# First sequence's gates and gate-weight sums placed inside the last FP4 down products, and its gate matrix by seven products

## The chip, the cores and the metric

The kernel runs as one launch on one core of a Trainium2 chip. The metric is the time of that launch on the device, in microseconds (us); the number given for a kernel is the median of several runs. For the kernel before that is 986.02 us, from three runs between 985.76 and 986.28 us.

## The reference, cut to what matters

Two layers follow each other on 2048 rows (two sequences of 1024 tokens) of 512 features. The first is linear attention and an FFN whose weights are packed FP4. The second is gated linear attention and an FFN that only the better half of the tokens passes. Each of the four steps ends in `x = layernorm(x + step(x))`. The change is at the seam between the FP4 FFN and the gated attention:

```python
# FP4 FFN (down part):      y = (silu(gate) * up) @ w_down.T ; y / rms(y)
# gated attention, per sequence:
q = softmax(x @ Wq.T); k = sigmoid(x @ Wk.T); v = x        # 32 features each
gf = log_sigmoid(-k)                                       # decay gates
o = gla_chunk(q, k, v, gf)                                 # chunked scan with state S
go = o @ Wog.T + x @ Wig.T                                 # the gate matrix, 512 x 1024
on = o * rsqrt(mean(o * o) + 1e-5) * g_norm_w
out = (on * silu(go)) @ Wo.T
```

`go` is one product of the 1024-wide pair (x, o) with the pair (Wig, Wog).

## The kernel before, in words

Rows are worked in four blocks of 512 tokens (blocks 0 and 1 are the first sequence, 2 and 3 the second). Weights and activations are fp32, and all products run on TensorE; a product of two 2 x 2 block matrices is done with seven block products instead of eight wherever the sums that this needs can be made beforehand by VectorE or GpSimd (Strassen's way, in Winograd's form). One fp32 matmul of the program shows as two MATMUL records in the trace.

**The FP4 stage (L688 to L944).** For each block `scaled_sums` (L690) makes gate and up from the unpacked weights `wgu` (45 KB in each partition), and `down` (L734) multiplies the result with `wdn` in products P1, P2, P5, P4, P6, P7, P3 and a rest P8, each ended by VectorE adds into `y`. The down products of a block lie inside the gate and up products of the next one; those of block 3 have nothing to lie in and stand alone, from about 509 to 552 us. The loop after `Wog` is loaded hands them out in seven portions, and between the portions it puts the transposes of block 1 (`turn`) and the 64 small matmuls `logits(0)` (L661), whose bank `lp` holds q and k of the first sequence before their nonlinearities. `Wig` and `Wog` are loaded at 494.6 and 509.3 us into rooms of their own. `old.rest()` and `now.rest()` (L855 on) are the row normalisations of blocks 2 and 3.

**The gated attention (from L945).** Here `fp4` is closed and its memory goes to new pools: `w34` (with `w1` and four rooms B0 to B3), `jk`, and `wk` (stage 3). `Gates` (L984) turns `lp` into q, k, the log decay `l` and its suffix sums `e`: activations Exp, Exp, Exp, Ln, Exp on ScalarE, seven VectorE operations between them, one matmul `ep` (L1008) and the product `kd` (L1011). It uses tiles of `wk`, so that it can't begin before the FP4 stage is over. `scores` (L1015) makes for one block the decays `ex` from a matmul `cp`, transposes q and k (`tp`), builds the masked score matrix A through `sc` and `sk`, a per-block decay through the small matmul `dp` (L1055), and the states S through four `up` matmuls. `attend` (L1083) makes o^T in 28 or 32 pairs of small matmuls (`op`), which ScalarE copies out and squares. `rms` (L1106) gives the row factors.

**The gate matrix.** Block 0 takes `plain_gate` (L1127): eight matmuls of 512 columns for each of four row groups, four with `Wig` (spread as fillers in `scores(0)`, which calls them by `beside`) and four with `Wog` after `attend`. Each group ends in a Silu and one VectorE operation. Blocks 1 to 3 take `gate` (L1144), which does the same by seven products of eight 256-column matmuls, with sums of the weights (`sums_of_gate`, L973, four VectorE operations of 1024 elements), of x and o (`x_sum`, `o_sum`, `other_sums`). In the trace these weight sums lie between 583 and 593 us. `finish_by_seven` and `finish` multiply by `W1o` and add to x; `scored_rows` normalises and scores the rows, `route` ranks them.

**What sets the order.** The order in the program is not the order on the engines: a scheduler places every instruction by its own estimate of when its inputs are there, and `tc.issue_after(ins)` holds a group back behind an instruction. Each engine then works its list strictly in order. PSUM banks are handed out in rings (`mm` and `acc`, four banks each here), so a matmul can also wait for the reader of the bank's last tile.

Of the kernel before, what the change touches and what calls it, by code (L numbers as in the profile page):

```python
# [10 lines left out]
F32 = mybir.dt.float32  # L11
# [62 lines left out]
def body(ctx: ExitStack, tc: tile.TileContext, a: dict, out: bass.AP):  # L74
# [147 lines left out]
    wgu = wfp4.tile([P, KC, 2 * I_FF], F32R, name="wgu")  # L222
# [446 lines left out]

    with tc.tile_pool(name="s2", bufs=1) as wk2:  # L670
# [137 lines left out]
        class Normed:  # L808
# [12 lines left out]
            def squares(self, part):  # L821
                for i in part:
                    nc.scalar.activation(junk, self.y[:, i], AF.Square, accum_out=self.ms[:, i : i + 1])

            def power(self):
                ms = self.ms
                nc.gpsimd.tensor_scalar(ms, ms, 1.0 / C, 1e-6, ALU.mult, ALU.add)
                nc.gpsimd.tensor_tensor(ms, ms, const("mhalf"), ALU.pow)
# [26 lines left out]
            def rest(self):  # L855

                for i in range(4):
                    x = x_t[self.blk][:, i]
                    nc.vector.scalar_tensor_tensor(x, self.y[:, i], self.ms[:, i : i + 1], x, ALU.mult, ALU.add)
                    row_stats(self.mv[:, i], x)  # L860
                    yield
                layernorm(x_t[self.blk], self.mv)
# [56 lines left out]
        load_w(Wog, "WogT")  # L919
        rings["mm"], rings["acc"] = range(4), range(4, 8)  # L920
# [3 lines left out]
        for n, steps in enumerate((11, 12, 10, 12, 10, 10, 14)):  # L924
# [4 lines left out]
            if n == 2:  # L929
                lp = logits(0)  # L930
        now.squares(range(4))
        now.power()
# [8 lines left out]
    w1 = w34.tile([P, KC, DFF], F32, name="w1")  # L941
    nc.sync.dma_start(out=w1, in_=a["w1"].rearrange("(k p) f -> p k f", p=P))
    load_w(W1o, "W1oT")
    nc.sync.dma_start(out=rw, in_=a["rw"].to_broadcast([P, C]))  # L944
    nc.sync.dma_start(out=b2, in_=a["b2"].to_broadcast([P, C]))  # L945
# [3 lines left out]

    def part(i, shape, name):  # L950

        return w34.tile([P, *shape], F32, tag=f"B{i}", name=name)
# [8 lines left out]


    gA11, gA12, gA21, gA22 = (
        w.rearrange("p k (m e c) -> p k m e c", e=2, c=P)[:, :, :, e] for e in range(2) for w in (Wig, Wog)
    )
    gsums = [part(i, [2, KC, 256], f"gsums{i}") for i in range(3)]
    gS1, gS2, gS4 = (
        gsums[i // 2][:, i % 2].rearrange("p k (m c) -> p k m c", c=P) for i in range(3)
    )
    T1, T2, T4 = gsums[1][:, 1], gsums[2][:, 0], gsums[2][:, 1]  # L970
    gS3 = gA21

    def sums_of_gate():  # L973
        nc.vector.tensor_add(gS1, gA21, gA22)
        nc.vector.tensor_sub(gS2, gS1, gA11)
        nc.vector.tensor_sub(gS3, gA11, gA21)
        nc.vector.tensor_sub(gS4, gA12, gS2)

# [5 lines left out]
    class Gates:  # L984


        def __init__(self, lp):
            lg = lp.rearrange("p (i d) -> p i d", d=64)
            q, k, l, e = (wk.tile([P, 8, 32], F32, tag=n, name=n) for n in ("q3", "k3", "l3", "e3"))
            kd = wk.tile([P, 8, 4, 32], F32, tag="kd", name="kd")  # L990
            self.q, self.k, self.l, self.kd = q, k, l, kd

            nc.scalar.activation(k, lg[:, :, 32:], AF.Exp, scale=-1.0)
            nc.vector.tensor_scalar_add(k, k, 1.0)
            nc.vector.reciprocal(k, k)
            nc.scalar.activation(l, k, AF.Exp)
            nc.scalar.activation(l, l, AF.Ln, bias=const("one"))
            red = sp.tile([P, 8], F32, tag="red", name="red")
            nc.vector.tensor_reduce(red, lg[:, :, :32], AX.X, ALU.max)
            nc.vector.tensor_sub(q, lg[:, :, :32], red.unsqueeze(2).to_broadcast([P, 8, 32]))  # L1000
            nc.scalar.activation(q, q, AF.Exp)
            den = sp.tile([P, 8], F32, tag="den", name="den")
            nc.vector.tensor_reduce(den, q, AX.X, ALU.add)
            nc.vector.reciprocal(den, den)
            nc.vector.tensor_mul(q, q, den.unsqueeze(2).to_broadcast([P, 8, 32]))

            ep = mm_bank("ep")
            nc.tensor.matmul(ep[:, :256], const("suf"), l.rearrange("p i d -> p (i d)"), start=True, stop=True)  # L1008
            nc.scalar.activation(e.rearrange("p i d -> p (i d)"), ep[:, :256], AF.Exp)

            nc.vector.tensor_mul(  # L1011
                kd, e.unsqueeze(2).to_broadcast([P, 8, 4, 32]), k.unsqueeze(2).to_broadcast([P, 8, 4, 32])
            )

    def scores(blk, gates, beside=None):  # L1015

        part = slice(4 * (blk % 2), 4 * (blk % 2) + 4)

        def flat(x):
            return x[:, part].rearrange("p i d -> p (i d)")  # L1020

        cp = mm_bank("cp")[:, : 3 * P]
        nc.tensor.matmul(cp, flat(gates.l), const("cm"), start=True, stop=True)
        ex = wk.tile([P, 4, P], F32, tag="ex", name="ex")
        nc.scalar.activation(ex[:, :3].rearrange("p e t -> p (e t)"), cp, AF.Exp)
        nc.scalar.activation(ex[:, 3], cp[:, :P], AF.Exp, scale=-1.0)
        tp = mm_bank("tp")
        nc.tensor.transpose(tp[:, :P], flat(gates.q), ident)  # L1030
        nc.tensor.transpose(tp[:, P : 2 * P], flat(gates.k), ident)
# [6 lines left out]

        last = sp.tile([P, 4], F32, tag="own", name="last")
        nc.vector.tensor_scalar_mul(last, own, ex[:, 2, P - 1 :])  # L1040
# [12 lines left out]
        dp = mm_bank("dp")  # L1053
        with tc.issue_after(beside(0)) if beside else contextlib.nullcontext():
            nc.tensor.matmul(dp[:, :4], const("quads"), last, start=True, stop=True)  # L1055
        decay = sp.tile([P, 4], F32, tag="decay", name="decay")
        nc.vector.tensor_copy(decay, dp[:, :4])
        sc = mm_bank("sc")
        with tc.issue_after(beside(1)) if beside else contextlib.nullcontext():
            nc.tensor.matmul(sc, km, qm.rearrange("p i t -> p (i t)"), start=True, stop=True)  # L1060
# [22 lines left out]
    def attend(blk):  # L1083

        A, qi = tri[blk]
        o = oT[blk] = wk.tile([P, KC, 512], F32, tag="oT", name="oT")
# [27 lines left out]
    def x_sum(blk):  # L1114
        nc.vector.tensor_sub(T1, xT[blk][:, :, 256:], xT[blk][:, :, :256])

    def o_sum(blk):
        nc.vector.tensor_sub(T2, oT[blk][:, :, 256:], T1)

    def other_sums(blk):  # L1120
        x, o = xT[blk], oT[blk]
        nc.vector.tensor_sub(x[:, :, 256:], o[:, :, 256:], x[:, :, 256:])
        nc.vector.tensor_sub(T4, o[:, :, :256], T2)

    banks, last_3 = [], [None]

    def plain_gate(m, first):  # L1127

        cut = slice(m * P, (m + 1) * P)
        if first:  # L1130
            banks.append(acc_bank("go"))
            for k in range(KC):
                ins = nc.tensor.matmul(banks[m], Wig[:, k, cut], xT[0][:, k], start=k == 0, stop=False).ins
            return ins
        else:
            for k in range(KC):
                nc.tensor.matmul(banks[m], Wog[:, k, cut], oT[0][:, k], start=False, stop=k == KC - 1)
            if m == 0:
                uT[0] = place_w(3, "uT")
            sil = wk.tile([P, 512], F32, tag="sil", name="sil", bufs=2)  # L1140
            nc.scalar.activation(sil, banks[m], AF.Silu)
            nc.vector.scalar_tensor_tensor(uT[0][:, m], oT[0][:, m], gw[:, m : m + 1], sil, ALU.mult, ALU.mult)

    def gate(blk):  # L1144


        u = uT[blk] = uT[0]
        c = u.rearrange("p (m e) (s t) -> p m e s t", e=2, s=2)
        c11, c12, c21, c22 = (c[:, :, e, s] for e in range(2) for s in range(2))
        x = xT[blk]  # L1150

        def product(ps, w, b, half, first):
            with tc.issue_after(last_3[0]):
# [25 lines left out]
        nc.scalar.copy(c11, product(one, gA11, x, 0, True))  # L1179
        yield  # L1180
        p5 = product(two, gS1, T1, 0, True)
        yield
        nc.scalar.copy(c22, p5)
        yield
        nc.scalar.copy(c12, product(one, gS2, T2, 0, False))
        p2 = product(acc_bank("go"), gA12, oT[blk], 0, True)
        yield nc.vector.tensor_add(c11, c11, p2).ins
        p7 = product(one, gS3, x, 1, False)
        yield nc.vector.tensor_add(c22, c22, p7).ins
        nc.vector.tensor_add(c12, c12, product(two, gS4, oT[blk], 1, False))  # L1190
        yield end(0)
        nc.scalar.activation(c21, product(one, gA22, T4, 0, False), AF.Silu)
# [3 lines left out]
    def sums_of_W1o():  # L1196
        W1oT = part(3, [4, 512], "W1oT")
# [217 lines left out]
    def finish_ffn(w2, h):  # L1415
# [59 lines left out]
        def steps(b):  # L1475
# [4 lines left out]
            c11 = wk.tile([P, 512], F32, tag="c11", name="c11")  # L1480
# [91 lines left out]
    gates = Gates(lp)  # L1572

    def fillers(h):

        turn(2, (2 * h, 2 * h + 1))
        plain_gate(2 * h, True)
        return plain_gate(2 * h + 1, True)

    scored = scores(0, gates, fillers)  # L1580
    with tc.issue_after(scored):
        for _ in ending:
            pass
        sums_of_gate()
        x_sum(1)
    for blk in range(NB):
# [146 lines left out]
```

## Time and profile before

| what | us |
|---|---|
| median of the runs shown | 986.02 |
| the profiled execution's own time | 985.74 |
| its span, first to last instruction | 983.8 |
| TensorE matmul busy | 967.1 (98%) |
| VectorE busy | 697.6 (71%) |
| ScalarE busy | 290.3 (30%) |
| GpSimd busy | 302.9 (31%) |
| block 3's last down product ends, the stage changes | 551.65 |
| the first product of `finish_by_seven` for block 0 begins | 611.07 |

The page of the profile gives busy time of each engine and the costliest groups. The waits view lists for each engine which line waited for which. The timeline gives, for a window, merged runs of one kind of instruction: its start, how long it ran, engine, line, operation, `out<-in` by tile names, shape, count, and in brackets the idle time before it and what ended that. PE is TensorE, DVE VectorE, ACT ScalarE, POOL GpSimd, SP the queue that starts DMAs.

### The profile page before, as it was taken

Reading aid. Unit: us, or ns where it says so; the run is one execution under the profiler, and the core shown is the slowest. Engines: PE = TensorE matmul, PEld = TensorE weight load, DVE = VectorE, ACT = ScalarE, POOL = GpSimd, SP = SyncE. Lnnn points to the kernel's source line nnn. Section 1 sums busy time; section 2 is a strip of 40 time slices with the busy share of each in tenths; the row PEclk is TensorE's granted clock in tenths of the full one; section 3 lists DMA queues with packets and bytes.
Section 4 is the critical chain, followed back from the end, with each engine's and each line's share of the span. In section 5 each row is a group of like instructions: output and inputs, shape, how many; then the busy total and the mean of one; then the engine's idle time right before and its main releaser. Section 6 shows DMA issues by size and latency. Waiting matters only on the chain. (4 is left out here: it accounts for less than half of the span.)

```text
span 983.8 us, 11753 instructions
## 1 busy us (share of the span) xinstructions
PE 967.1 (98%) x4373; PEld 768.5 (78%) x4373; DVE 697.6 (71%) x1340; ACT 290.3 (30%) x496; POOL 302.9 (31%) x276
## 2 busy tenths in 40 slices
PE   9999999999999999999999999999999999999996
PEld 6668876785888888888889656979768588888885
DVE  3569986987975686686672566565897795789644
ACT  2344323333542272263240442132221123220000
POOL 1110282005887265575565022001032011000022
PEclk9999999999999999999999999999999999999999
DMA  9632222100000000000020500000004302140011
GB/s 333 194 88 74 87 69 64 49 1 1 1 1 1 1 1 1 1 11 1 0 86 1 224 1 1 1 1 1 1 33 139 128 17 70 44 171 1 1 43 43
DMA packets 25979, 48.85 MB, mean 50 GB/s; under 512 B 4684, under 2 KB 6732, under 8 KB 25411
## 3 DMA queue, kind: packets, MB, share of 16 engines
q1 hardware_dynamic: 23283, 42.98, 13.2%
q0 software_dynamic: 1920, 4.22, 1.1%
q10 hardware_dynamic: 720, 0.92, 0.3%
q8 instruction: 34, 0.56, 0.2%
q14 instruction: 22, 0.18, 0.1%
HBM read 39.70 MB, written 10.52 MB: 51 GB/s over the span
## 5 line engine op out<-in xcount | busy, mean ns | idle before, releaser
L181 POOL TENSOR_TENSOR rs<-rs,table 128x4 f32<-128x4 f32 (+1 forms) x21 | 20.3, 967 | 301.3 <-DVE rs L180 301.0
L709 DVE SCALAR_TENSOR_TENSOR gate<-gatep,scale,gate 128x512 f32<-128x512 f32 x123 | 91.5, 744 | 7.4 <-PE gatep L698 6.9
L709 DVE SCALAR_TENSOR_TENSOR up<-upp,scale,up 128x512 f32<-128x512 f32 x112 | 83.2, 743 | 0.2
L698 PE MATMUL gatep<-x1Th,wgu 128*128 128x512 f32 x176 | 73.1, 415 | 0.6 <-DVE x1Tl L212 0.6
L698 PE MATMUL upp<-x1Th,wgu 128*128 128x512 f32 x176 | 70.4, 400 | 0.1
L698 PE MATMUL gatep<-x1Tl,wgu 128*128 128x512 f32 x176 | 69.6, 395 | 0.0
L698 PE MATMUL upp<-x1Tl,wgu 128*128 128x512 f32 x176 | 69.5, 395 | 0.0
L703 ACT ACTIVATE gate<-gatep,scale 128x512 f32<-128x512 f32 x41 | 28.3, 690 | 112.1 <-PE gatep L698 105.7
L745 PE MATMUL P<-wdn,h 128*128 128x256 f32 x256 | 60.5, 379 | 0.0
L898 POOL TENSOR_TENSOR h<-up,gate 128x512 f32<-128x512 f32 x30 | 38.6, 1286 | 69.6 <-ACT gate L897 64.5
L745 PEld LDWEIGHTS P<-wdn,h 128*128 128x128 f32 x256 | 48.5, 190 | 6.7
L1103 POOL TENSOR_TENSOR sum<-sum,sq 128x512 f32<-128x512 f32 x12 | 18.0, 1499 | 101.6 <-issue 77.1
L367 PE MATMUL xk<-pair,x 128*128 128x512 f32 x96 | 42.7, 592 | 0.0
L188 DVE BATCH_NORM_STATS2 st<-x 128x6 f32<-128x512 f32 x64 | 41.9, 677 | 0.4
L698 PEld LDWEIGHTS upp<-x1Th,wgu 128*128 128x128 f32 x176 | 33.0, 188 | 10.6 <-DVE up L709 2.4
L698 PEld LDWEIGHTS gatep<-x1Th,wgu 128*128 128x128 f32 x176 | 33.1, 188 | 8.8 <-DVE gate L709 1.1
L698 PEld LDWEIGHTS upp<-x1Tl,wgu 128*128 128x128 f32 x176 | 33.1, 188 | 7.6 <-issue 0.2
L698 PEld LDWEIGHTS gatep<-x1Tl,wgu 128*128 128x128 f32 x176 | 33.1, 188 | 6.9
L1463 PE MATMUL yp<-w,h 128*128 128x256 f32 x168 | 37.7, 379 | 0.0
L745 PE MATMUL P<-T,S 128*128 128x256 f32 x160 | 35.8, 379 | 0.0
L1463 PEld LDWEIGHTS yp<-w,h 128*128 128x128 f32 x168 | 31.9, 190 | 4.3
L1377 ACT ACTIVATE h<-h,b 128x512 f32<-128x512 f32 x28 | 18.4, 713 | 57.2 <-DVE h L1401 34.6
(459 smaller groups left out, 2325.0 us busy)
## 6 DMA issues: line engine op xcount, KB each, us to landing
pk<-in_gu SPq DMA_DIRECT2D x16, 352.0 KB, 3.8
x<-in_x SPq DMA_DIRECT2D x4, 1024.0 KB, 13.1
w<-in_w SPq DMA_DIRECT2D x1, 4096.0 KB, 14.0
xs<-picked SPq DMA_DIRECT2D x4, 1024.0 KB, 5.1
out<-x SPq DMA_DIRECT2D x4, 1024.0 KB, 4.3
w<-in_w SPq DMA_DIRECT2D x4, 1024.0 KB, 7.0
x0T<-in_xT SPq DMA_DIRECT2D x3, 1024.0 KB, 7.1
pk<-in_dn SPq DMA_DIRECT2D x11, 256.0 KB, 3.4
```

What stands on the lines that cost most here:

```text
L181: power = nc.gpsimd.tensor_tensor(rs[:, :n], rs[:, :n], const("mhalf")[:, :n], ALU.pow).ins
L188: nc.vector.bn_stats(st, x)
L367: ins = nc.tensor.matmul(acc_of[b][c], x_t[blk][:, i, c * P : (c + 1) * P], pairs_of["k", blk][i // 2][:, i % 2], start=blk % 2 == 0 and i ...
L698: ins = nc.tensor.matmul(ps, wgu[:, k, at * P : (at + 1) * P], x[:, k], start=x is parts[0], stop=x is parts[1]).ins
L703: nc.scalar.activation(acc, ps, AF.Copy, scale=s)
L709: last = nc.vector.scalar_tensor_tensor(acc, ps, s, acc, ALU.mult, ALU.add).ins
L745: last_p[0] = nc.tensor.matmul(cut, x(j)[:, r], w[:, j], start=j == 0, stop=j == NP - 1 and tail is None).ins
L898: hm = nc.gpsimd.tensor_mul(h.chunk(f), up, gate).ins
L1103: nc.gpsimd.tensor_add(sum2, sum2, sq)
L1377: nc.scalar.activation(x, x, AF.Gelu_apprx_tanh, bias=b1[:, f : f + 1])
L1463: nc.tensor.matmul(ps[:, 256 * r : 256 * r + 256], x(r, j), w(j), start=j == 0, stop=j == NJ - 1)
```

## The change

Nine edits, all in one diff:

1. `wgu` moves from the pool `wfp4` into the outer weights pool under the tag `big`; after its last use the same memory is one tile `big`, which holds the rooms B0 to B3 (`part`), one room for `kd` and one for o^T (`o_room`). They are there before the FP4 stage is closed.
2. `Gates` is made inside the FP4 stage, after the third portion, in the rooms `b2` and `rw`; its `kd` and the four sums of gate weights follow after the fourth portion, and x_sum of block 0 after the fifth.
3. The squares of block 3's `y` and their root go behind `scores(0)`'s first half, into a tile of `jk`.
4. The loads of `rw` and `b2` go into block 0's turn of the loop, and W1o's load is issued ahead of w1's.
5. `scores` is split: `front` (the matmul `cp`, the decays, `dp`) can be called earlier. It is, for blocks 1 and 3, ahead of `attend` of the block before.
6. `plain_gate` is removed; block 0 uses `gate(0)`. Its first two products are the fillers in `front(0)` and `scores(0)`; o's products follow `attend(0)`, in an order of its own.
7. `rms(0)` and the end of block 3's normalisation go behind `scores(1)`.
8. `sums_of_W1o` is tied behind the scores of block 1.
9. The tile `c11` of the last stage and one of the four h tiles use rooms in `big`.

```diff
-    wgu = wfp4.tile([P, KC, 2 * I_FF], F32R, name="wgu")
+    wgu = wpool.tile([P, KC, 2 * I_FF], F32R, tag="big", name="wgu")
...
+    class Gates:
+        def __init__(self, lp, rooms):
+            lg = lp.rearrange("p (i d) -> p i d", d=64)
+            self.q, self.k, self.l, self.e = q, k, l, e = rooms
...
+        def decayed(self, kd):
+            self.kd = kd
+            nc.vector.tensor_mul(
+                kd, self.e.unsqueeze(2).to_broadcast([P, 8, 4, 32]), self.k.unsqueeze(2).to_broadcast([P, 8, 4, 32])
+            )
...
+        big = wpool.tile([P, 4 * 2048 + 3072], F32, tag="big", name="big")
...
+        gsums = [part(i, [2, KC, 256]) for i in range(3)]
+        W1oT = part(3, [4, 512])
+        kd_room, o_room = shaped(8192, [8, 4, 32]), shaped(9216, [KC, 512])
...
             if n == 2:
-                lp = logits(0)
-        now.squares(range(4))
-        now.power()
+                gates = Gates(logits(0), [
+                    x[:, i * 256 : (i + 1) * 256].rearrange("p (i d) -> p i d", d=32) for x in (b2, rw) for i in range(2)
+                ])
+            if n == 3:
+                gates.decayed(kd_room)
+                sums_of_gate()
+            if n == 4:
+                x_sum(0)
...
+    load_w(W1o, "W1oT")
     nc.sync.dma_start(out=w1, in_=a["w1"].rearrange("(k p) f -> p k f", p=P))
-    load_w(W1o, "W1oT")
-    nc.sync.dma_start(out=rw, in_=a["rw"].to_broadcast([P, C]))
-    nc.sync.dma_start(out=b2, in_=a["b2"].to_broadcast([P, C]))
...
+    def front(blk, gates, before=None):
         cp = mm_bank("cp")[:, : 3 * P]
-        nc.tensor.matmul(cp, flat(gates.l), const("cm"), start=True, stop=True)
+        nc.tensor.matmul(cp, of_tiles(gates.l, blk), const("cm"), start=True, stop=True)
...
-            if m == 0:
-                uT[0] = place_w(3, "uT")
-            sil = wk.tile([P, 512], F32, tag="sil", name="sil", bufs=2)
-            nc.scalar.activation(sil, banks[m], AF.Silu)
-            nc.vector.scalar_tensor_tensor(uT[0][:, m], oT[0][:, m], gw[:, m : m + 1], sil, ALU.mult, ALU.mult)
...
+        if blk == 0:
+            ins = p2()
+            p3 = p3()
+            nc.scalar.copy(c12, product(one, gS2, gT2, 0, False))
+            yield ins
+            nc.vector.tensor_add(c12, c12, p3)
+            yield end(0)
+            yield p7()
...
-    gates = Gates(lp)
+    gating = gate(0)
     def fillers(h):
         turn(2, (2 * h, 2 * h + 1))
-        plain_gate(2 * h, True)
-        return plain_gate(2 * h + 1, True)
-    scored = scores(0, gates, fillers)
+        next(gating)
+        return last_3[0]
+    front(0, gates, lambda: fillers(0))
+    scored = scores(0, gates, lambda: fillers(1))
+    first_ex = last_ex[0]
+    front(1, gates)
+    with tc.issue_after(first_ex):
+        now.squares(range(4), jk.tile([P, C], F32, tag="junk", name="junk"))
+    now.power()
     with tc.issue_after(scored):
-        for _ in ending:
-            pass
-        sums_of_gate()
-        x_sum(1)
+        next(ending)
     for blk in range(NB):
...
+        if blk == 2:
+            front(3, gates)
+        sum2 = attend(blk)
...
         if blk == 0:
-            for m in range(1, KC):
-                plain_gate(m, False)
-            continue
+            o_sum(0)
+            with tc.issue_after(scored):
+                W1o_sums = sums_of_W1o()
+            nc.sync.dma_start(out=rw, in_=a["rw"].to_broadcast([P, C]))
+            nc.sync.dma_start(out=b2, in_=a["b2"].to_broadcast([P, C]))
         other_sums(blk)
+        if blk == 0:
+            for _ in ending:
+                pass
...
+            if n == blk == 0:
+                rms(0, sum2)
...
-            c11 = wk.tile([P, 512], F32, tag="c11", name="c11")
+            c11 = shaped(8192 + 512 * b, [512])
...
-    h = [[wk.tile([P, 4, 512], F32, name=f"h0{g}", bufs=1) for g in range(4)]]
+    h = [[*(wk.tile([P, 4, 512], F32, name=f"h0{g}", bufs=1) for g in range(3)), o_room]]
```

## The prediction, made before the run

> **What bounds the kernel now.** I read the page first (busy shares), then TensorE's rows in the waits view, then its timeline from 509 to 611 us, where the change lies, and last VectorE's, ScalarE's and GpSimd's timelines there.
>
> ```profile
> PE 967.1 (98%) x4373; PEld 768.5 (78%) x4373; DVE 697.6 (71%) x1340; ACT 290.3 (30%) x496; POOL 302.9 (31%) x276
> ```
>
> TensorE is the bound: only two things can shorten the kernel, fewer matmul columns or fewer gaps between matmuls. The waits view has the gaps:
>
> ```profile
> PE ep L1008 <- ACT l L997: 1.8, 2, 1.3
> PE dp L1055 <- DVE last L1040: 1.5, 2, 1.2
> PE hp L1384 <- ACT row L1352: 1.1, 1, 1.1
> PE rp L1297 <- DVE score L1280: 0.9, 1, 0.9
> PE up L1072 <- DVE decay L1057: 0.4, 1, 0.4
> PE x2Tp L197 <- ACT e L1009: 0.4, 1, 0.4
> PE mp L1109 <- POOL sum L1103: 0.3, 1, 0.3
> ```
>
> The reader is to see that four of the seven rows have their largest wait in the stretch of the first sequence; `hp` and `rp` belong to a later stage that the change leaves alone. The timeline of TensorE shows where, and gives the price of a matmul:
>
> ```profile
> 551.65 6.17 PE L1133 MATMUL go<-x2T,Wig 128*128 128x512 f32 x14
> 559.08 0.70 PE L1008 MATMUL ep<-l,table 128*128 128x256 f32 x2 [1.25 <-ACT l L997]
> 559.61 0.81 PE L1025 MATMUL cp<-table,l 128*128 128x384 f32 x2
> 560.77 0.66 PE L197 MATMUL x2Tp<-table,x 128*128 128x128 f32 x4 [0.35 <-ACT e L1009]
> ...
> 565.55 5.32 PE L1133 MATMUL go<-x2T,Wig 128*128 128x512 f32 x12
> 570.70 1.02 PE L1060 MATMUL sc<-qm,km 128*128 128x512 f32 x2
> ...
> 582.02 3.60 PE L1137 MATMUL go<-oT,Wog 128*128 128x512 f32 x8
> 585.92 1.05 PE L1109 MATMUL mp<-table,sum 128*128 128x1 f32 x8 [0.30 <-POOL sum L1103]
> ...
> 587.78 5.32 PE L1137 MATMUL go<-oT,Wog 128*128 128x512 f32 x12
> 594.27 0.36 PE L1055 MATMUL dp<-last,table 128*128 128x4 f32 x2 [1.17 <-DVE last L1040]
> ...
> 614.52 3.62 PE L1156 MATMUL go<-x2T,Wig 128*128 128x256 f32 x16
> 617.98 1.89 PE L1224 MATMUL grow<-W1oT,uS 128*128 128x256 f32 x8
> ```
>
> Durations overlap, so I price by the distance of starts: 565.55 to 570.70 for 12 records of 512 columns is 0.429 us each; 614.52 to 617.98 for 16 records of 256 columns is 0.216 each. So a column costs the same in both shapes.
>
> **What the skill says.** (1) Perfetto Trace Analysis, Identifying the Most-Contended Engine: matmul busy share is a poor measure of how near TensorE is to its limit. The trace agrees in that its durations overlap (5.32 us shown for 5.15), so I use starts. (2) ScalarE: Activation LUTs, What ACT_TABLE_LOAD costs: a load takes about 1283 ns plus a drain of about 1380. The trace has the 1.28 us (557.22 to 558.50) but the next activation starts 0.02 later; the measurement decides. (3) SBUF, Who interferes with whom: VectorE and GpSimd share a port pair under an exclusive lock. The trace agrees: x_sum (L1115) takes 1.22 us alone and 2.19 beside a GpSimd add, a GpSimd S operation (L760) 0.73 alone and 1.09 beside VectorE.
>
> **The change, part by part.** I compare 551.65 (P8's end) to 611.07 (first W1o product): 59.42 us.
>
> *Gaps in it.* ep: 551.65 + 14 x 0.429 = 557.66, it starts 559.08: 1.42. x2Tp after cp: 559.61 + 0.65 (cp's distance at 647.09) = 560.26 to 560.77: 0.51. mp: 582.02 + 8 x 0.429 = 585.45 to 585.92: 0.47. dp: 587.78 + 12 x 0.429 = 592.93 to 594.27: 1.34. Together 3.74 us. All four have a cause that the change removes: ep, e and cp's input are made earlier, dp of block 1 gets its input ahead of attend(0), mp goes behind other products.
>
> *Seven products.* plain_gate is 32 matmuls, 64 records x 0.429 = 27.46 us. gate(0) is 7 x 8 matmuls, 112 records x 0.2157 = 24.16. That is 3.30 us less, on TensorE, so on the path.
>
> *ep* (0.53, 559.08 to 559.61) only moves from this stretch into the down products: nil. cp of blocks 1 and 3 (0.65 each) moves ahead: nil.
>
> *VectorE's part.* Removed from 553 to 593: seven gate operations (about 5.2), kd 1.22, four weight sums 4.9; they move to 510 to 543. New: x_sum, o_sum, two other sums for block 0, 4 x 1.22, and three adds of 0.69, 6.9 us. All this costs nothing while TensorE has work in its list, and each place must be tested.
>
> *Inside the down products.* In the order in which the changed program is built (the built order below) x_sum(0) stands between VectorE's last two `up` operations, so the last chunk of h comes up to 2.2 us late: GpSimd multiplies it at about 512.5 to 513.5 instead of 511.92, and TensorE reads it at 516.43, so hidden. Then VectorE: four x operations to 517.2 to 518.2, statistics 2.8, gS1 and gS2 to 522.3 to 523.3, then `rs` to GpSimd, which here stands ahead of GpSimd's 15 S operations; they end at 524.5 + 15 x 1.09 = 541 against 533.5, and P3 reads the last at 545.6: hidden by 4 us. The normalisation, gS3 and gS4 (1.2 to 2.2 each) and one y add end at 528.5 to 531.5. The logits end at 531.8, so the gates' chain can start at once. From 639.97 (k's Exp for the second sequence) the same chain to ep took 6.6, of which 1.3 was ScalarE held by another copy; the first took 553.75 to 559.08, 5.33. So ep is ready at 531.9 + 5.33 = 537.2. In the built order TensorE has it after one P6 matmul, at 536.97 + 0.43 = 537.4. It just fits: I take 0.2 us, bounds 0 and 1.5 (VectorE held by the port pair up to a microsecond longer). Queued behind ep are nine P6 matmuls and P7, P3, P8.
>
> *After P8.* Count from E, its new end. cp 0.65, eight transposes 0.87, product 1 3.45, then dp, two transposes, eight more 1.2, product 5 3.45: sc at E + 9.7. VectorE has qm at E + 7.3 and ScalarE the 3.3 us of squares from E + 2.7, read by GpSimd's root and then VectorE at E + 16: all hidden. Call sc's start Z. As before, sc, sk, four `up` take 5.1, then cp 0.7; attend 6.25 and dp 0.2: op ends at Z + 12.2. VectorE follows `up` to Z + 6.7, then `last`, decay and four x operations of block 3 (to 9.6), W1o sums and statistics, km, kk, q4 to Z + 14.2 to 15.0, o_sum to 15.4 to 17.2, qm to 16.0 to 17.8. TensorE wants q4's bank at 14.6, and qm at 16.4: waits of 0 to 0.5 and 0 to 1.5. The spread is GpSimd's squares sum (from Z + 10.2), which can double each VectorE operation of two SBUF inputs. Then P3 and c12's product follow without a wait, and P7 and A22's product find their sums a microsecond early. I take 1.0 us for new waits after P8, bounds 0 and 4 (the ends above, and as much again in A22's and W1o's inputs).
>
> *Later.* front(3) makes block 3's decay early, which removes the 0.43 of `up` behind `decay`. In the FFN 21 VectorE sums of 0.38 us (8.0) move from after 879 to between 831 and 879, where the windows view leaves VectorE 12.5 us idle: hidden; I take 0.3, bounds 0 and 1. A gain there is excluded, since TensorE has no gap after 842 until 960.
>
> *DMAs and queues.* SP: W1o ahead of w1 is how they were already issued (550.16 and 551.90). rw and b2 are loaded once q and k of block 1 are transposed, near 575; rw's load took 10.2 us, and its first reader is at 637. Wig and Wog are issued as before, and the second has landed by 515 (DMA share), before gS1 at 520. GpSimd's memset of `cnt` passes eight scatters, 0.07 us. Table loads fall from six to four in the stretch, on ScalarE, which waits for TensorE there: nil. `big` costs no copies, and its first writer waits for the last wgu matmul at 509.2, before VectorE is there.
>
> **Sum.** -3.74 - 3.30 + 0.2 + 1.0 - 0.43 + 0.3 = -5.97. The profiled execution took 985.74 (span 983.8, 1.94 around it), so 979.8; it is 0.28 below the median, so I predict 980.0 for the median.
>
> **The rivals.**
> *The waits come back* (chance 0.27). VectorE between Z + 9 and Z + 20 has 13 operations and GpSimd three adds on the same ports. If q4 and qm take the upper ends (0.5 + 1.5), the third `up` and A22's product wait as much, and ep 0.5, new waits are about 4.5: 986.0 - 7.5 + 0.3 + 4.5 = 983.3. For it: dp waited for VectorE in this very place. Against it: VectorE gives up 11.3 us of work in this stretch and takes 6.9 of new.
> *Only a trace of it is left, within 0.2%* (0.08): the gates come too late for P6 by 4 us and block 1 keeps its waits: -7.5 + 6.5 = -1.0, 985.0. A change that does not do what it says is excluded by the built order, which has the gates between the down products.
> *Slower* (0.07). One mechanism: ep stands in TensorE's list ahead of P6's rest, and its chain stands on VectorE behind x_sum, the four sums and a normalisation that itself waits for GpSimd. Every microsecond by which VectorE reaches the gates after 532.4 is lost on TensorE, and `rs` delays GpSimd's S operations that P7 and P3 read. It decides from 7.3 us, that is if VectorE is there after about 539.7 instead of 528.5 to 531.5. At 10 us late: 986.0 - 7.0 + 10 = 989. Against it: it needs every sum at 2.2 us and the statistics doubled too.
>
> **How the numbers follow.** The forecast (980.0, its own range 978.3 to 981.8) has 0.58. All new waits at nil give 986.0 - 7.5 = 978.5; I set the low end at 978.3. The high end, 983.4, takes in nearly all of the first rival and leaves out the other two: about 0.18 is outside. A measurement of this kernel tells about 0.2%, 2 us, from no change: faster 0.85, same 0.08, slower 0.07.
>
> **What would show it.** Right: P8 to W1o's first product about 53 us instead of 59.42; ep between P6's matmuls with a gap below half a microsecond; no dp and no mp in TensorE's waits in that stretch; 256-column `go` records only; the `up` wait behind decay gone. Wrong: a gap at ep of several microseconds with VectorE or ScalarE named; sc or `up` of block 1 waiting for VectorE by over 2 us in all; new gaps after 842.

## The result, and the profile after

The changed kernel takes 979.17 us (median of 6 runs, 977.99 to 979.85) against 986.12 for the kernel before (6 runs beside them): a ratio of 0.9931, 95% interval 0.9921 to 0.9941. It is faster by 0.7%. Its profiled execution has a span of 977.5 us, the one of before 983.8.

TensorE is still the bound. Its share in the page has not moved, which shows how little that share says: there are 4421 matmul records, 48 more than before, since the first block's gate is now 112 records of 256 columns in place of 64 of 512.

```profile
PE 962.0 (98%) x4421; PEld 776.0 (79%) x4421; DVE 707.6 (72%) x1347; ACT 289.2 (30%) x496; POOL 305.4 (31%) x276
```

TensorE's rows of the waits view (waited in total, times, longest):

```profile
PE hp L1407 <- ACT row L1375: 1.1, 1, 1.1
PE dp L1055 <- DVE last L1052: 1.1, 1, 1.1
...
PE rp L1320 <- DVE score L1303: 0.9, 1, 0.9
...
PE ep L692 <- ACT l L681: 0.5, 1, 0.5
PE sc L1090 <- DVE qm L1083: 0.5, 1, 0.5
...
PE ep L692 <- ACT rw L681: 0.3, 1, 0.3
```

Of before's rows `x2Tp`, `mp` and `up` are gone, `ep` and `dp` have one large wait less, and `sc` is new. The row of `dp` is not the one that the prediction removed: the timeline of TensorE has it at 643 us, in the second sequence, where the kernel before waited 0.33.

```profile
536.25 0.70 PE L692 MATMUL ep<-rw,table 128*128 128x256 f32 x2 [0.27 <-ACT rw L681]
...
551.03 0.81 PE L1046 MATMUL cp<-table,rw 128*128 128x384 f32 x2
...
552.55 3.62 PE L1163 MATMUL go<-x2T,Wig 128*128 128x256 f32 x16
556.01 0.28 PE L1055 MATMUL dp<-last,table 128*128 128x4 f32 x2
...
578.04 1.12 PE L1090 MATMUL sc<-qm,km 128*128 128x512 f32 x2 [0.52 <-DVE qm L1083]
...
588.84 0.95 PE L1139 MATMUL mp<-table,sum 128*128 128x1 f32 x8
...
603.78 1.89 PE L1247 MATMUL grow<-W1o,uT 128*128 128x256 f32 x8
...
643.33 0.39 PE L1055 MATMUL dp<-last,table 128*128 128x4 f32 x2 [1.05 <-DVE last L1052]
```

Marks on TensorE's timeline say where the 6.3 us of the span went (us, from one mark to the next in the two profiled executions):

| stretch | before | after | difference |
|---|---|---|---|
| start to first gate product (`gatep`) | 217.98 | 217.89 | -0.09 |
| to P1 of block 3 | 291.41 | 289.92 | -1.49 |
| to W1o's first product (`grow`) | 101.68 | 95.97 | -5.71 |
| to the second sequence's logits | 21.15 | 21.30 | +0.15 |
| to the first `hp` of the FFN | 144.48 | 145.09 | +0.61 |
| to the first of the last 32 matmul records | 191.60 | 191.59 | -0.01 |
| to the end of the span | 15.5 | 15.7 | +0.2 |

The third row is what the prediction worked out. The second and the fifth it had not: a gain ahead of the place of the change, and a loss behind it. The last row differs from one execution to another: it is 15.5 again in `dose1` below, which has the last stage of the changed kernel.

### The profile page after: what moved, and what is told of

Same layout as the page of the kernel before. It is cut to its first block, busy times and chain, and to the rows that moved or that the text cites. A ratio compares the mean times of both kernels' runs of the same rounds, so it can differ in the third digit from the quotient of the medians.

```text
span 977.5 us, 11854 instructions
## 1 busy us (share of the span) xinstructions
PE 962.0 (98%) x4421; PEld 776.0 (79%) x4421; DVE 707.6 (72%) x1347; ACT 289.2 (30%) x496; POOL 305.4 (31%) x276
## 5 line engine op out<-in xcount | busy, mean ns | idle before, releaser
L1163 PE MATMUL go<-big 128*128 128x256 f32 x192 | 43.4, 380 | 0.0
L1163 PEld LDWEIGHTS go<-big 128*128 128x128 f32 x192 | 36.2, 190 | 4.8
L777 PEld LDWEIGHTS P<-T,S 128*128 128x128 f32 x160 | 30.3, 190 | 4.2
```

Source lines behind the costliest of these rows:

```text
L777: last_p[0] = nc.tensor.matmul(cut, x(j)[:, r], w[:, j], start=j == 0, stop=j == NP - 1 and tail is None).ins
L1163: ins = nc.tensor.matmul(ps[:, 256 * m : 256 * m + 256], w[:, k, m], b[:, k, 256 * half : 256 * half + 256], start=first and m == 0 and k ...
```

## Experiments

The ratios are to runs of the kernel before on the same chip; its median beside them was 985.65 (`addr`, `plain`, `late_gates`, `both`), 986.05 (`pad32`, `pad64`, `dose`), 985.73 (`dose1`, `dose3`) and 985.69 (`after2`, `best`). `after2` is the changed kernel again. Lateness "by starts" below is, as in the prediction, the distance from one start to the next beyond what a matmul of that shape takes elsewhere (0.216 us for a record of 256 columns); the idle time in brackets is some 0.16 smaller. Where two kernels differ by less than 0.3%, the marks decide: between two profiles of the changed kernel the interval from P1 to `grow` came out as 95.97 and 96.00, the one from `gatep` to P1 as 289.92 and 289.86.

| kernel | time (us) | ratio to before, 95% interval | `gatep` to P1 | P1 to `grow` | second logits to `hp` |
|---|---|---|---|---|---|
| before | 985.65 | | 291.41 | 101.68 | 144.48 |
| addr | 984.11 | 0.9983, 0.9977 to 0.9990 | 289.86 | 101.66 | 144.48 |
| pad32 | 984.72 | 0.9989, 0.9982 to 0.9995 | 290.12 | 101.65 | 144.48 |
| pad64 | 985.61 | 0.9996, 0.9987 to 1.0005 | 291.27 | 101.67 | 144.49 |
| plain | 982.01 | 0.9964, 0.9951 to 0.9978 | 289.90 | 98.90 | 145.10 |
| late_gates | 981.56 | 0.9964, 0.9951 to 0.9978 | 289.85 | 98.33 | 145.10 |
| after2 | 979.50 | 0.9937, 0.9923 to 0.9950 | 289.86 | 96.00 | 145.09 |
| dose1 | 979.90 | 0.9939, 0.9922 to 0.9956 | 289.87 | 96.35 | 145.09 |
| dose3 | 985.29 | 0.9992, 0.9983 to 1.0001 | 289.92 | 102.18 | 145.10 |
| dose | 988.22 | 1.0023, 1.0016 to 1.0030 | 289.98 | 105.54 | 145.10 |
| both | 977.52 | 0.9920, 0.9907 to 0.9934 | 289.90 | 95.28 | 144.28 |
| best | 977.36 | 0.9914, 0.9901 to 0.9928 | 289.95 | 94.85 | 144.28 |

**The two halves of the change.** `plain` keeps the early gates and gives the first block its old gate:

```
-                sums_of_gate()        # at n == 3
...
-                x_sum(0)              # at n == 4
...
-    gating = gate(0)
+    gating = plain_gate()             # 4 groups of 8 matmuls, 512 columns
...
-            o_sum(0)
...
+                sums_of_gate()        # behind W1o's sums
```

> The changed kernel with its early gates, but with the first block's gate from plain products of 512 columns (32 matmuls, 64 records), and the sums of gate weights made after them. Sum theory: 64 x 0.429 against 112 x 0.2157 is 3.3 us more, less the 0.5 us of sc waiting behind o_sum, which isn't there: 979.2 + 2.8 to 3.3 = 982.0 to 982.5; P8's end to W1o's first product 55.5 to 56.1 instead of 52.75. Rival (the products gain nothing, their sums' waits eat it, and all of the gain is from the order): 979.2, stretch 52.8.

Measured: 982.01 us, and P1 to `grow` 2.93 us longer than in the changed kernel. The products are worth what the count of columns says, less two waits. By starts `ep` is 0.20 late here, since VectorE comes to the gates without the four sums, and 0.43 in the changed kernel; an `up` and `sc` of block 1 are 0.25 and 0.31 late here, `sc` alone 0.68 there. So of the 3.30 are left 3.30 - 0.23 - 0.12 = 2.95. The rival, that the products gain nothing, is out.

`late_gates` keeps the seven products and gives the gates their old place:

```
-                gates = Gates(logits(0), [...])   # at n == 2
+                lp = logits(0)
...
+        with tc.issue_after(last_p[0]), tc.issue_after(last_y[0]):
+            gates = Gates(lp, [...])
+            gates.decayed(kd_room)
```

> The changed kernel with seven products, but the gates' chain on VectorE and ScalarE held until VectorE has added P8, so that ep comes after the down products as in the kernel before. Sum theory: the gaps ep 1.42 and x2Tp 0.51 come back and the 0.27 in P6 goes: 979.2 + 1.7 = 980.9, ep with a gap of 1 to 2 us. If the chain's later parts (decay, kd, q) come late too: up to 982.5. Rival (where the gates stand is worth nothing, since TensorE has product 1 to do meanwhile): 979.2, no gap at ep.

Measured: 981.56 us, P1 to `grow` 2.36 us longer than in the changed kernel. `late_gates` on TensorE's timeline:

```profile
555.71 0.70 PE L692 MATMUL ep<-rw,table 128*128 128x256 f32 x2 [1.15 <-ACT rw L681]
556.25 0.81 PE L1049 MATMUL cp<-table,rw 128*128 128x384 f32 x2
557.88 0.98 PE L197 MATMUL x2Tp<-table,x 128*128 128x128 f32 x7 [0.82 <-ACT rw L693]
```

The two waits of before are back, by starts 1.31 and 0.99 us (1.42 and 0.51 there). TensorE had product 1 to do meanwhile, 3.5 us, and that was not enough: `ep` came 5.7 us after the end of the down products at 550.0. The sum theory had 1.7; `x2Tp` waits twice as long as before, and block 0's `dp` is 0.3 late too. The rival, that the place of the gates is worth nothing, is out.

So the order without the products (`plain`) is worth 101.68 - 98.90 = 2.78 us, and the products on top of it 2.93; together they are the 5.71. The early place of the gates alone is worth 2.36 of that, with all else as in the changed kernel. `late_gates` keeps the early `front` and the late `rms`, so the waits of block 1's `dp` and of `mp` are gone in it; no run has the products in the order of before, and what they would gain there is not shown.

**The gain ahead of the change.** TensorE's instructions between 218 and 508 us are the same, in the same order. The first edit of the diff does one thing there: `wgu` is taken from another pool, so its address is 117,024 bytes into a partition instead of 118,976, and the small statistics tiles lie behind it instead of ahead. `addr` makes only that edit, with what has to follow it (the later sums cut from the tile that takes `wgu`'s place):

```
-    wgu = wfp4.tile([P, KC, 2 * I_FF], F32R, name="wgu")
+    wgu = wpool.tile([P, KC, 2 * I_FF], F32R, tag="big", name="wgu")
```

> The kernel before with the change's memory layout alone: wgu lies in the pool of the later tiles (tag big), and the weight sums, W1o sums, kd, oT and c11 are cut from a tile that takes its place afterwards. Order of work and products as before. Theory A (where the unforeseen 1.5 us between the first gate product at 218 us and P1 of block 3 at 508 us came from: wgu's new address): the interval from the first gatep to P1 of block 3 falls from 291.4 to about 289.9 us and the time from 986.1 to about 984.6. Theory B (the interval differs from execution to execution, or hangs on something else in the change): the interval stays at 291.4 and the time at 986.1.

Measured: 984.11 us and 289.86: theory A. The groups of TensorE in the kernel before between 218 and 508 us (busy, mean ns of one, idle before):

```profile
L698 PE MATMUL gatep<-x1Th,wgu 128*128 128x512 f32 x175 | 72.7, 415 | 0.6 <-DVE x1Tl L212 0.6
L698 PE MATMUL upp<-x1Th,wgu 128*128 128x512 f32 x175 | 70.0, 400 | 0.1
L698 PE MATMUL gatep<-x1Tl,wgu 128*128 128x512 f32 x175 | 69.2, 395 | 0.0
L698 PE MATMUL upp<-x1Tl,wgu 128*128 128x512 f32 x175 | 69.1, 395 | 0.0
```

The same groups of `addr`:

```profile
L698 PE MATMUL gatep<-x1Th,wgu 128*128 128x512 f32 x176 | 72.5, 412 | 0.6 <-DVE x1Tl L212 0.6
L698 PE MATMUL upp<-x1Th,wgu 128*128 128x512 f32 x176 | 70.3, 400 | 0.1
L698 PE MATMUL gatep<-x1Tl,wgu 128*128 128x512 f32 x176 | 68.9, 392 | 0.0
L698 PE MATMUL upp<-x1Tl,wgu 128*128 128x512 f32 x176 | 68.9, 391 | 0.0
```

No wait has gone. In three of the four groups the mean record is 3 or 4 ns shorter; the fourth has 400 ns in both. There are 704 records in all; the window cuts off the last of the kernel before. The old address is a multiple of 64 bytes, the new one 32 more than a multiple. Two kernels tell the address from the neighbours:

```
+    wfp4.tile([P, 8], F32, name="pad")     # pad32; [P, 16] in pad64
     wgu = wfp4.tile([P, KC, 2 * I_FF], F32R, name="wgu")
```

> The kernel before with an unused tile of 32 bytes per partition ahead of wgu, so that wgu (and the tiles behind it) begin 32 bytes later, at an address that is 32 modulo 64 as in the changed kernel, while the small statistics tiles stay where they were. Theory A1 (wgu's address within 64 bytes sets the rate of the gate and up products): the interval from the first gate product to P1 of block 3 is 289.9 us instead of 291.4, the time 984.5. Theory A2 (it is the place of the small tiles, or wgu's place in a larger unit): the interval stays at 291.4, the time at 986.

Measured: 290.12 us in the interval, 1.29 of the 1.49 gained, and 984.72 in all.

> The kernel before with an unused tile of 64 bytes per partition ahead of wgu, so that wgu's address is 0 modulo 64 as in the kernel before. Theory A1 (the address within 64 bytes): the interval stays at 291.4 us, the time at 986. Theory A3 (any other address than the old one helps, in units of 128 bytes or more): 289.9 and 984.5.

Measured: 291.27 and 985.61. So theory A1: 32 bytes more give the gain, 64 bytes more don't, with the statistics tiles in their old place in both. The other operand's tiles (`x1Th`, `x1Tl`) lie at 32 past a multiple of 64 in all these programs, so whether `wgu`'s own offset counts or its match with theirs is not told apart. Other offsets were not tried. `wdn` moved by the same bytes in both kernels, and the down products' matmuls stayed at a mean of 379 ns, so it is not a rule for every matmul.

**The price of coming late to the gates.** The slower rival says that each microsecond by which VectorE reaches the gates late is lost at `ep`. Extra subtractions, whose result nobody reads, were put between the fourth sum and the gates' first addition:

```
+                for _ in range(6):              # dose3: 3, dose1: 1
+                    more = nc.vector.tensor_sub(gsums[2][:, 1].rearrange("p k (m c) -> p k m c", c=P), gS1, gS2).ins
...
+            with tc.issue_after(before) if before else contextlib.nullcontext():   # before is more
+                nc.vector.tensor_scalar_add(k, k, 1.0)
```

> As above with one more subtraction. Theory: 1.75 less 0.65 plus 0.27: a gap of about 1.4 us at ep, no fall of the clock, P1 of block 3 to W1o's first product 1.1 us longer than 95.97, time 980.3. Rival (VectorE was earlier at the gates than it seems, so that one more is free): gap 0.3, time 979.2.

> As the kernel with six more VectorE subtractions ahead of the gates, but with three, and ep in the same place of TensorE's list as in the changed kernel. Theory: three times 1.75 us beside GpSimd less 0.65 that VectorE was early, plus 0.27: a gap of about 4.9 us at ep (3.2 if each takes 1.2). If a gap this long costs no more than itself, P1 of block 3 to W1o's first product is 4.6 us longer than the changed kernel's 95.97; if the granted clock falls to half some 3 us into the gap, as it did with six, and stays there for some microseconds after it, the interval is 6 to 7.5 us longer. Time 983.2 to 986.5.

> The changed kernel with six more VectorE subtractions of 1024 elements, whose result nobody reads, between the normalisation with the weight sums and the first gates' addition; ep stands four P6 matmuls (1.7 us) later in TensorE's list. Theory (the prediction's slower rival: each microsecond by which VectorE comes late to the gates is lost on TensorE at ep): six times 1.2 us alone or 1.75 beside GpSimd, less 0.65 that VectorE was early and 1.7 by which ep stands later, plus the 0.27 of before: a gap of 5.1 to 8.4 us at ep and a time of 984 to 987.5. Rival (the products that stand behind ep are taken ahead of it, or the gates' late part has room): gap below 2 us, time 979 to 981.

Measured: gaps at `ep` of 0.63, 3.96 and 6.92 us, and 979.90, 985.29 and 988.22 us in all. `dose`, with six, ran first; its time lies above the 984 to 987.5 that were expected, and its trace had the clock at half, so that `dose3` has this as one of its theories. `dose1` missed its 1.4: the subtraction took 1.75, but VectorE then had no wait for ScalarE (0.65), and the gates' addition took 0.28 instead of 0.86. Of its 1.75 us 0.37 reached `ep`. In `dose3` `ep` is 3.70 us later after P1 than in the changed kernel, yet the interval to `grow` is 6.21 longer; with six it is 8.38 later, of which 1.72 is its later place, and the interval 9.57 longer. The difference is TensorE's granted clock, in `dose3` by stretches (length, busy time of PE, PEld, DVE, ACT, POOL with instructions, granted clock, DMA share, GB/s):

```profile
538.00:539.00 1.00, 0.00 (x0) 0.00 (x0) 0.49 (x3) 0.89 (x3) 1.00 (x3) 0.97 0.00 0
539.00:540.00 1.00, 0.00 (x0) 0.00 (x0) 0.98 (x3) 1.00 (x1) 0.38 (x1) 0.50 0.00 0
...
544.00:545.00 1.00, 1.00 (x4) 0.82 (x3) 0.00 (x0) 0.00 (x0) 0.00 (x0) 0.50 0.00 0
545.00:546.00 1.00, 1.00 (x4) 0.79 (x4) 0.00 (x0) 0.00 (x0) 0.00 (x0) 0.61 0.00 0
546.00:547.00 1.00, 1.00 (x7) 0.87 (x6) 0.00 (x0) 0.00 (x0) 0.00 (x0) 1.00 0.00 0
```

TensorE ran dry at 536.6, the clock fell to half at about 538.9, and `ep` at 540.69 and the matmuls behind it ran at half speed until 545.8: 5.1 us at half speed is 2.5 lost, and 3.7 + 2.5 is the 6.2. The Trainium skill, TensorE: Matmul & The Clock Gate, under "What's actually happening", has the mechanism: the array's clock goes to half after an idle window of about 3.4 us, and back after a busy one of that length. The trace agrees in the half and in the kind of wait that brings it about; but here it fell after 2.4 us of idling, sooner than the page has it, and came back 5.1 us after the first matmul. The measurement decides. The gaps of the kernel before, none over 1.4 us in this stretch, didn't bring it about: its clock is 1.00 from 551 to 605 us.

**The loss behind the change.** In the second sequence `e3`, before a tile of its own, is now one of the two junk tiles. ScalarE's timeline in the kernel before, from l's Ln on:

```profile
646.00 0.51 ACT L997 ACTIVATE l<-l,table 128x256 f32<-128x256 f32 x1
646.52 1.28 ACT L1009 ACT_TABLE_LOAD   x1
```

The same two rows of the changed kernel:

```profile
638.85 0.51 ACT L681 ACTIVATE l<-l,table 128x256 f32<-128x256 f32 x1
640.19 1.28 ACT L693 ACT_TABLE_LOAD   x1 [0.83 <-PE ep L692]
```

The load of the table for e's Exp used to run while TensorE made `ep`; now it waits for `ep`. In the built program the activation has a second wait, for GpSimd's last reading of the junk tile, and its wait for `ep` stands as an instruction of its own ahead of the load. The Trainium skill, ScalarE: Activation LUTs, What ACT_TABLE_LOAD costs, calls the load an instruction of the engine's own; so it stands in ScalarE's list, and a wait ahead of it delays it, here by the 0.83 us of the second row. `both` undoes that, and also puts the first block's sums behind `qi` of the second block, for the wait at `sc`:

```
-                jk.tile([P, 8, 32], F32, tag="junk", name="e3"),
+                wk.tile([P, 8, 32], F32, tag="e3", name="e3"),
...
-            o_sum(0)
+            with tc.issue_after(last_qi[0]):
+                o_sum(0)
...
+        with tc.issue_after(last_qi[0]) if blk == 0 else contextlib.nullcontext():
             other_sums(blk)
```

> The changed kernel with two edits: the second sequence's e3 has a tile of its own again instead of a junk tile, so that the table load for e's Exp has no wait ahead of it, and the first block's o_sum and other sums stand behind qi of the second block's scores on VectorE. If the two waits are what they seem: dp of block 2 waits 0.3 instead of 1.05 us, sc of block 1 doesn't wait: 979.2 - 0.7 - 0.5 = 978.0. Rival (the time goes into the next wait, at sc or up of block 2 and at c12's product of block 0): 979.2.

Measured: 977.52 us. ScalarE's timeline of `both`:

```profile
637.84 0.51 ACT L681 ACTIVATE l<-l,table 128x256 f32<-128x256 f32 x1
638.36 1.28 ACT L693 ACT_TABLE_LOAD   x1
```

And the row of block 1's `sc` on TensorE's:

```profile
576.62 1.11 PE L1090 MATMUL sc<-qm,km 128*128 128x512 f32 x2
```

The load has no wait, `dp` waits 0.23, and logits to `hp` is 0.81 shorter; `sc` doesn't wait, and P1 to `grow` is 0.69 shorter. Neither wait moved on to a next one. `best` moves one thing more: `ep` is held behind one more P6 matmul.

> The kernel with the two edits (e3 in its own tile, the first block's sums behind qi), and ep one P6 matmul (0.43 us) later in TensorE's list, nothing else moved. Theory: the gap of 0.27 at ep goes: P1 of block 3 to W1o's first product 95.0 us instead of 95.28 with the two edits and 95.97 in the changed kernel, time 977.3. Rival (ep's later end delays cp or kd): 95.28 or more.

Measured: 977.36 us (975.92 to 977.77), and 94.85 from P1 to `grow`; `ep` doesn't wait. Of the two edits and this one the last is too small to be seen in the time, but the three together are: the changed kernel was run again beside it.

> The changed kernel again, beside the next one on the same chip. Theories: if the address of wgu, and not the single execution, sets the rate of the gate and up products, the interval from the first gate product to P1 of block 3 is 289.9 us again, and P1 to W1o's first product 95.97; time 979.2.

Measured: 979.50 us (979.19 to 980.16), 289.86 and 96.00. The runs of the two don't overlap, so `best` beats both kernels, the changed one by 2.1 us.

## Why the prediction was right, and where it was wrong

The time, 979.17, is 0.8 under the 980.0 predicted. In the stretch that the prediction worked out, its mechanism held, and the sum with it: 5.84 forecast, 5.71 measured. Outside it two terms were missed, -1.5 and +0.7; that the total still came so close is in part luck, since they have opposite signs.

- *Gaps removed, -3.74, and seven products, -3.30.* Right: without the products the order is worth -2.78, which is the four gaps less 0.20 at `ep`, 0.56 at `up` and `sc` of block 1 and 0.22 at the first `op` behind `cp`; the products on top of it are worth -2.93, the 3.30 less some 0.35 of waits behind their sums. P8's end to `grow` is 52.75 us, predicted "about 53".
- *ep in P6, +0.2.* Right in kind, but twice the size: 0.43 by starts (0.27 in the idle column), and `best`, which has no such wait, is 0.43 shorter than `both`. TensorE was there when forecast, 28.0 us after P1; the chain was ready after 28.4 us instead of 27.8.
- *New waits after P8, +1.0.* Right in size: by starts 0.68 at `sc` (0.52 in the idle column; `both`, without it, is 0.69 shorter) and 0.22 at the first `op` behind `cp`. It was the place that the prediction named: `qm` behind `o_sum`, which took 2.04 us beside GpSimd's sums.
- *`up` behind decay, -0.43.* Only half right. The wait is gone, but block 3's `sc` and `sk` start 0.3 and 0.1 late in its place, with no releaser named in the trace, and small matmuls that stand elsewhere now have starts a tenth late. Logits to `hp` in `both`, where `dp` waits as little as before, is 0.20 shorter than before, 0.10 of it at `dp`.
- *Sums of h, +0.3.* Nothing: the FFN's stretch is 191.59 against 191.60. (The windows view of before leaves VectorE 11.5 us idle from 831 to 879, not 12.5; the 8.0 fit in either.)
- *Missed: -1.5 from wgu's address.* The step "`big` costs no copies, and its first writer waits for the last wgu matmul" looked at the new tenant of the room and not at the old one's address. The premise that only fewer columns or fewer gaps can shorten the kernel left no room for it: these are the same columns at a higher rate. The views of before don't show addresses, but moving a matmul's operand belongs in the range.
- *Missed: +0.7 at the second sequence's `dp`.* "Table loads fall from six to four in the stretch, on ScalarE, which waits for TensorE there: nil" counted the loads of the first sequence and passed over `e3`'s new room in the second, where a load hides behind `ep` only as long as it waits for nothing.
- *The slower rival.* Its mechanism is real: VectorE late at the gates shows at `ep`. Its price was not: "every microsecond" is too much for the first 1.75, of which `dose1` lost a fifth, and too little in the gaps of 3.96 and 6.92 us, in which the clock fell. It decides from about 4 us of gap (`dose3`, equal to before), not 7.3 (or the 7.0 of the prediction's own sum for 10 us); six subtractions are slower than before, 1.0023.

The sum of the terms was 5.97 us and the span fell by 6.3; the -1.5 hides that the later stretches lost 0.75 where 0.13 of gain was forecast. Left open: what the late starts of a tenth behind single small matmuls wait for, why an address changes the rate, and which offsets besides 32 bytes are good ones.

## What to carry to other kernels

Price a reordering by gaps on the bounding engine's timeline and a cheaper algorithm by its columns: each came within 1 us of its price (2.78 for 3.74, 2.93 for 3.30), and the rest went into new waits for VectorE. When an edit changes where a tile lives, look at what else it changes: the instruction that inherits a wait (here a table load) and the address that a matmul reads. A wait on TensorE of up to 1.4 us cost itself here, one of 4 us cost 6, since the clock fell in it.

## What the runs showed of the hardware that was not expected

- The address of the weights of the gate and up products (fp32r, 128 x 512) sets their rate: at 32 bytes past a multiple of 64 the mean `x1Tl` record takes 391 to 393 ns, on the multiple 395; 1.2 to 1.5 us over 704 records.
- An idle TensorE was given half the clock after 2.4 us (`dose3`) and kept it for 5.1 us of work, 2.5 us lost on top of a gap of 3.96. With six extra subtractions it fell about 2.8 us into the gap and came back 5.9 us after the first matmul behind it.
